# Key and value biases carried by tokens plus one, and new costs and shifts in the list schedule of a convolution, attention and expert kernel

## The chip, the cores and the metric

The kernel runs on one core of one Trainium2 chip. The metric is the device time of one execution in microseconds (us). All arithmetic is in fp32.

## The reference, cut to what matters

The input x has 32 images of 128 channels and 64 x 64 pixels. Layer 0 normalises groups of channels, convolves by a learned butterfly transform, and adds the result to x. Layer 1 takes each image as 4096 tokens of 128 channels. It adds attention over channels and then a mixture of eight experts, of which each token uses two. The part that the change touches is the attention:

```python
def _L1_attn_ref(x, Wk, bk, Wv, bv):
    k = x @ Wk.T + bk
    v = x @ Wv.T + bv
    scores = jnp.einsum('sbe,sbf->sef', k, v)
    probs = jax.nn.softmax(scores / jnp.sqrt(jnp.float32(seq_len)), axis=-1)
    return jnp.einsum('sef,sbf->sbe', probs, x)
...
t = t + _L1_attn_ref(_ln_t(t), L1_attn_Wk, L1_attn_bk, L1_attn_Wv, L1_attn_bv)
```

The "sequence" of this attention is the batch of one image's tokens: k and v have 128 features, and the scores are the 128 x 128 matrix k^T v, summed over the 4096 tokens. So with G the sum over tokens of the outer product of a normalised token with itself (the Gram matrix), the scores are Wk G Wv^T plus terms with the biases and with the sum of the tokens. A normalised token (`_ln_t`) has mean zero over its 128 channels.

## The kernel before, in words

The kernel has three phases. The first (until about 900 us in the trace) normalises and transforms the images, the second (until about 2560 us) mixes channels for each frequency, and the third, from line 727, does the inverse transform, the attention and the experts. Only the third is changed. Its work is written as small pieces for each image b, handed to a planner (`Plan`, lines 28 to 81) by `add` (line 805).

A piece has an engine, a cost in us, a due time, pieces that must be over before it, and counted resources that it takes or frees: `tl` (three PSUM banks for small products), `pe` (three PSUM banks for experts), `cv` (one PSUM tile of the inverse transform), `tm` (two buffers of gated expert outputs), `x`, `r`, `xg`, `xn`, `xT` and so on. `Plan.run` is a list schedule: it advances a clock by the costs, and when an engine is free it issues the ready piece with the earliest due time. The order that comes out is the order of the instructions on each engine; the chip then runs each engine's instructions in that order, with semaphores between engines. The costs and due times thus set nothing but an order. The due time is `SLOT` (114 us) times a position in images, plus an entry of `SHIFT` (line 797) by the piece's name, so a larger shift puts a piece later in rank.

For image b the pieces of the third phase are, in order of the data:

- `w`, `wo`, `h`, `ho` (lines 833 to 884): the inverse transform on PE into `cv`, copies `u` on ACT (line 848), and the addition onto the image `y` on DVE (line 868).
- `pt`, `to`, `sa` (913 to 942): four transposes at a time on PE turn the image to tokens, ACT copies them to `tk`, DVE takes statistics. `tk` has two buffers by b % 2, so `pt` of b waits for the output transposes `st` of b-2 (line 940).
- `va`, `pwa`, `na` (895 to 950): moments on DVE, a power on POOL (tile `m`, line 911), and minus mean times the reciprocal deviation on DVE (line 948, `nmr`).
- `xg`, `pg` (954 to 979): ACT writes the normalised tokens, a group of four blocks of 128 tokens at a time, and PE adds up the Gram matrix over 32 blocks. The buffers `xg` have a 129th column of ones, so the product of 128 x 129 also holds the sum of the tokens.
- `gs`, `pa`, `rows`, `pb`, `t1`, `pb2` (981 to 1008): DVE copies the Gram matrix to `gs`. `pa` is three matmuls that make two rows on one partition: the sum of the tokens, and that sum times Wv plus 4096 times the value bias (`ntok` holds 4096). DVE copies them to `rows`. `pb` is the Gram matrix times Wv plus an outer product of the first row and the value bias (lines 998 and 999, the second with a contraction of one row); DVE copies it to `t1`; `pb2` multiplies by Wk and adds an outer product of the key bias and the second row (1007 and 1008).
- `sm`, `pr`, `sr`, `sn`, `pc`, `prx` (1010 to 1049): the softmax, its transpose, and its product with the router weights.
- `pp`, `at`, `ad` (1052 to 1101): the attention's output by PE, scaled on ACT with `rstd` and `nmr`, added to `tk` on DVE, with statistics again.
- `vb`, `pwb`, `lg`, `nb` and `l2` to `gt` (1113 to 1175): the second power on POOL, router logits and the gates of the two best experts, on DVE.
- `xn`, `px`, `xT` (1180 to 1203), `pe` (line 1209, 64 for each image), `m` (the gated product `tm`, DVE line 1220), `s` (sums over experts on POOL, lines 1245 to 1248), `st` and `so` (transpose and store). In the last image five pairs of blocks are weighed on DVE alone (line 1232).

The set-up (lines 736 to 792) loads the weights on ACT's queue and takes the mean over input channels out of the expert weights, adding a 128th of the expert bias: with `nmr` of the experts raised by one (line 1126), tokens plus one times these weights give the product and the bias. The experts therefore already work in the way that the change brings to key and value.

Of the kernel before, what the change touches and what calls it, by code (L numbers as in the profile page):

```python
# [16 lines left out]
P = 128  # L17
# [73 lines left out]
def kernel(  # L91
# [644 lines left out]
    ct = ctx.enter_context(tc.tile_pool(name="ct", bufs=1))  # L736
    wk_sb = ct.tile([P, P], F32, name="wk_sb")
    nc.scalar.dma_start(wk_sb, wkT)
    wv_sb = ct.tile([P, P], F32, name="wv_sb")
    nc.scalar.dma_start(wv_sb, wvT)  # L740
    bk_sb = ct.tile([1, P], F32, name="bk_sb")
    nc.scalar.dma_start(bk_sb, bk.unsqueeze(0))
    bv_sb = ct.tile([1, P], F32, name="bv_sb")
    nc.scalar.dma_start(bv_sb, bv.unsqueeze(0))
    rb_sb = ct.tile([P, NE], F32, name="rb_sb")
# [6 lines left out]
    for e in range(NE):  # L752
        nc.gpsimd.memset(rank[:, e : e + 1], float(NE - e))
    ntok = ct.tile([1, 1], F32, name="ntok")
    nc.gpsimd.memset(ntok, float(NPIX))
    ones = ct.tile([P, P], F32, name="ones")
    nc.gpsimd.memset(ones, 1.0)

    NG = 4
    xg = [ct.tile([P, 4, P + 1], F32, name=f"xg{i}") for i in range(NG)]  # L760
    for t in xg:
        nc.gpsimd.memset(t[:, :, P : P + 1], 1.0)

# [8 lines left out]
    with tc.tile_pool(name="prep", bufs=1) as prep:  # L772

        ebb = prep.tile([P, NE, P], F32, name="ebb")
        nc.scalar.dma_start(
            ebb.rearrange("p e c -> p (e c)"), expert_b.rearrange("e c -> (e c)").partition_broadcast(P)
        )
        om = prep.tile([P, P], F32, name="om")
        nc.gpsimd.memset(om, 1.0 / P)
        for half in range(2):  # L780
            es = slice(4 * half, 4 * half + 4)
            pe = eps.tile([P, 512], F32, tag="pe", name=f"pm{half}")
            nc.tensor.matmul(pe, om, ew_sb[:, es, :].rearrange("d e c -> d (e c)"), start=True, stop=True)
            nc.vector.scalar_tensor_tensor(
                ebb[:, es, :].rearrange("p e c -> p (e c)"), ebb[:, es, :].rearrange("p e c -> p (e c)"),
                1.0 / P, pe, ALU.mult, ALU.subtract,
            )
        nc.vector.tensor_add(ew_sb, ew_sb, ebb)

        pe = eps.tile([P, 512], F32, tag="pe", name="pms")  # L790
        nc.tensor.matmul(pe[:, 0:NE], ones, prx[0][:, P + NE : QX], start=True, stop=True)
        nc.vector.tensor_copy(rws, pe[:, 0:NE])
# [4 lines left out]
    SHIFT = {  # L797
        "ad": 0.75, "at": -0.21, "f": 0.63, "gt": 0.63, "h": -0.15, "ho": -1.5, "l": 0.63, "lg": 0.15,
        "m": -0.08, "na": -0.08, "pe": 0.49, "pg": -0.45, "pt": -0.03, "pwa": -0.08, "pwb": 0.15,
        "r": -0.33, "s": 0.1, "sa": 0.33, "so": -0.09, "st": 0.47, "to": 0.52, "va": -0.08, "vb": 0.15,  # L800
        "wo": 0.12, "x": 0.44, "xT": 0.44, "xg": 0.12, "xn": 0.35,
    }
# [29 lines left out]
    def conv(b):  # L832
# [40 lines left out]
        for e in range(8):  # L873
            at = b + 0.08 * e
            add(b, f"w{e}", "PE", 1.8, at, w_inverse(e), [f"r{e}"] + [(b - 1, f"h{k}") for k in range(4)], ("cv",), ("r",))
            for oh in range(2):
                add(
                    b, f"wo{e}_{oh}", "ACT", 1.2, at, w_out(e, oh),
                    [f"w{e}"] + [(b - 1, f"h{k}") for k in range(4)], (), ("cv",) if oh else (),
                )  # L880
        for g in range(4):
            at = b + 0.68 + 0.07 * g
            add(b, f"h{g}", "PE", 2.15, at, h_inverse(g), [f"wo{e}_{oh}" for e in range(8) for oh in range(2)], ("cv",))
            add(b, f"ho{g}", "DVE", 1.25, at, h_out(g), [f"h{g}", "x"], (), ("cv",))

    def front(b):
# [8 lines left out]
        def moments(which):  # L895

            bs = v["bs"]
            even, odd = bs[:, :, 0, :], bs[:, :, 1, :]
            m2 = st.tile([P, 5, NT], F32, name=f"m2{which}_{b}", tag=f"m2{which}", bufs=2)
            total, diff, var, nmr, rstd = (m2[:, k, :] for k in range(5))  # L900
            nc.vector.tensor_add(total, even[:, :, 1], odd[:, :, 1])
# [36 lines left out]
        for g in range(8):  # L938
            at = s1 + 0.016 * g
            add(b, f"pt{g}", "PE", 0.55, at, turn(g), [(b - 2, f"st{g}")] + [f"ho{k}" for k in range(4)], ("tl",))  # L940
            add(b, f"to{g}", "ACT", 0.6, at, turned(g), [f"pt{g}"], (), ("tl",))
            add(b, f"sa{g}", "DVE", 1.15, at, stats1(g), [f"to{g}"] + (["sa0"] if g else []))
# [3 lines left out]
        def nmr1():  # L946
            total, var, nmr, rstd = v[1]
            nc.vector.scalar_tensor_tensor(nmr, total, -0.5, rstd, ALU.mult, ALU.mult)

        add(b, "na", "DVE", 0.9, s1 + 0.14, nmr1, ["pwa"])  # L950

        def norm(g):
            def run():
                total, var, nmr, rstd = v[1]
                for k in range(4):
                    i = 4 * g + k
                    nc.scalar.activation(
                        xg[g % NG][:, k, 0:P], t[:, i, :], AF.Identity, bias=nmr[:, i : i + 1], scale=rstd[:, i : i + 1]  # L960
                    )
            return run

        def gram(g):
            def run():
                if g == 0:
                    v["pg"] = tps.tile([P, 512], F32, tag="tl", name=f"pg{b}")
                for k in range(4):
                    i = 4 * g + k
                    nc.tensor.matmul(  # L970
                        v["pg"][:, 0 : P + 1], xg[g % NG][:, k, 0:P], xg[g % NG][:, k, :],
                        start=(i == 0), stop=(i == NT - 1),
                    )
            return run

        for g in range(8):
            at = s1 + 0.26 + 0.016 * g
            add(b, f"xg{g}", "ACT", 1.7, at, norm(g), ["na", (b if g >= NG else b - 1, f"pg{(g - NG) % 8}")], ("xg",))
            add(b, f"pg{g}", "PE", 1.06, at, gram(g), [f"xg{g}"] + ([f"pg{g - 1}"] if g else []), ("tl",) if g == 0 else (), ("xg",))

        def gsum():
            v["gs"] = st.tile([P, P + 1], F32, name=f"gs{b}", tag="gs")
            nc.vector.tensor_copy(v["gs"], v["pg"][:, 0 : P + 1])

        def rows_mm():
            pa, gs = tps.tile([P, 512], F32, tag="tl", name=f"pa{b}"), v["gs"]
            nc.tensor.matmul(pa[0:1, 0:P], gs[:, P : P + 1], ident, start=True, stop=True)
            nc.tensor.matmul(pa[0:1, P : 2 * P], gs[:, P : P + 1], wv_sb, start=True, stop=False)
            nc.tensor.matmul(pa[0:1, P : 2 * P], ntok, bv_sb, start=False, stop=True)
            v["pa"] = pa  # L990

        def rows_out():
            v["rows"] = st.tile([1, 2 * P], F32, name=f"rows{b}", tag="rows")
            nc.vector.tensor_copy(v["rows"], v["pa"][0:1, 0 : 2 * P])

        def kv1():
            pb = v["pb"] = tps.tile([P, 512], F32, tag="tl", name=f"pb{b}")
            nc.tensor.matmul(pb[:, 0:P], v["gs"][:, 0:P], wv_sb, start=True, stop=False)
            nc.tensor.matmul(pb[:, 0:P], v["rows"][:, 0:P], bv_sb, start=False, stop=True)

# [4 lines left out]
        def kv2():  # L1005
            pb = v["pb"]
            nc.tensor.matmul(pb[:, P : 2 * P], wk_sb, v["t1"], start=True, stop=False)
            nc.tensor.matmul(pb[:, P : 2 * P], bk_sb, v["rows"][:, P : 2 * P], start=False, stop=True)

# [28 lines left out]
        add(b, "gs", "DVE", 0.3, at, gsum, ["pg7"], (), ("tl",))  # L1038
        add(b, "pa", "PE", 0.9, at, rows_mm, ["gs"], ("tl",))
        add(b, "rows", "DVE", 0.42, at, rows_out, ["pa"], (), ("tl",))  # L1040
        add(b, "pb", "PE", 0.7, at, kv1, ["rows"], ("tl",))
        add(b, "t1", "DVE", 0.3, at, kv1_out, ["pb"])
        add(b, "pb2", "PE", 0.7, at, kv2, ["t1"])
        add(b, "sm", "DVE", 0.5, at, soft1, ["pb2"])
# [45 lines left out]
        for j, lo in enumerate(range(0, NT, 3)):  # L1090
            m = min(3, NT - lo)
            at = s1 + 0.45 + 0.016 * j
            add(b, f"pp{lo}", "PE", 0.3 * m, at, product(lo, m), ["prx", (b - 1, "lg")], ("tl",), ("x",) if lo == 30 else ())
            add(
# [82 lines left out]
    def experts(b):  # L1177
# [88 lines left out]
        for g in range(8):  # L1266
            at = s2 + 0.125 * g
            add(b, f"xn{g}", "ACT", 1.7, at - 0.1, normal(g), ["nb"], ("xn",))
            add(b, f"px{g}", "PE", 0.55, at - 0.05, turn(g), [f"xn{g}"], ("tl", "xT"), ("xn",))
            add(b, f"xT{g}", "ACT", 0.6, at - 0.05, turned(g), [f"px{g}"], (), ("tl",))  # L1270
            for k in range(4):
# [15 lines left out]
                elif k % 2:  # L1287
# [3 lines left out]
                    )  # L1291
            add(b, f"st{g}", "PE", 0.55, at + 0.25, back(g), [f"s{2 * g}", f"s{2 * g + 1}"], ("tl",))
            add(b, f"so{g}", "ACT", 0.6, at + 0.25, store(g), [f"st{g}"], (), ("tl",))
# [61 lines left out]
```

## Time and profile before

| | |
|---|---|
| median of three runs | 6177.5 us (6176.5 to 6183.15) |
| the profiled execution | 6179.07 us, span 6177.3 us, granted clock 0.99 |
| PE busy | 5988.3 us, 97% of the span |
| DVE, ACT, POOL busy | 4213.0, 3759.2, 4187.1 us |
| phase 1, 2 and the start of 3 | 0 to 900, 900 to 2560, 2560 to 2720 us |
| PE busy from 2560 to 2720 | 108.59 of 160 us |
| PE busy from 5600 to 6000, 6000 to the end | 382.24, 153.71 us |
| the Gram sum `pg` (lines 970, from 2700 on) | 1984 instructions, mean 275 ns |
| copies `gs`, `rows`, `t1` on DVE | mean 294, 412, 292 ns |
| `nmr` of the attention, line 948 | mean 558 ns |

In the profile, PE is TensorE, DVE is VectorE, ACT is ScalarE, POOL is GpSimd. Durations of PE instructions overlap, since matmuls are pipelined, so a mean is longer than what one adds to a busy stretch. One fp32 matmul is two instructions in the trace, and a transpose is one. Lines are named by the tile that is written, then those that are read: `pe<-ew_sb,xT`. Buffer numbers are left out, so one name stands for all images.

### The profile page before, as it was taken

The page shows a single profiled execution, that of the slowest core. Times are in us where ns is not written, and L with a number is a line of the kernel's source. Part 1 is how long each engine was busy: PE and PEld are TensorE (multiplying, and loading weights), DVE is VectorE, ACT ScalarE, POOL GpSimd, SP SyncE. Part 2 cuts the span into 40 slices and gives each one's busy share as a digit, 9 for nine tenths or more (in the row PEclk, how much of TensorE's full clock was granted, in tenths as well). Part 3 has the DMA queues.
Part 4 walks back from the last instruction along what each step waited for, and adds up shares of the span by engine and source line. Part 5 has one row for each costly group of instructions (what it writes and reads, how often), then busy time and mean ns, then how long its engine had stood idle before and what let it go on. Part 6 is the DMA issues. An engine that isn't in the chain of part 4 may idle for free. (4 is left out here: it accounts for less than half of the span.)

```text
span 6177.3 us, 218388 instructions
## 1 busy us (share of the span) xinstructions
PE 5988.3 (97%) x94922; PEld 4714.0 (76%) x94922; DVE 4213.0 (68%) x7686; ACT 3759.2 (61%) x7089; POOL 4187.1 (68%) x3755
## 2 busy tenths in 40 slices
PE   7999999999999999789999999999999999999988
PEld 7999998999999999666666666666666666666654
DVE  5565545555555555358778787787878778787777
ACT  7666654555555555376666666766667666666753
POOL 2110006666666666238888888888888888888888
PEclk9999999999999999899999999999999999999999
DMA  6766666666666666622222222222212222131100
GB/s 201 236 227 232 233 213 170 173 172 171 174 172 172 172 172 172 160 74 95 69 84 78 65 96 64 88 76 71 91 62 94 67 86 78 64 96 64 67 21 26
DMA packets 556965, 756.55 MB, mean 122 GB/s; under 512 B 58466, under 2 KB 321892, under 8 KB 551908
## 3 DMA queue, kind: packets, MB, share of 16 engines
q1 hardware_dynamic: 554096, 741.38, 39.9%
q8 instruction: 745, 12.21, 0.9%
q14 instruction: 216, 1.77, 0.1%
q10 hardware_dynamic: 1908, 1.19, 0.1%
HBM read 406.80 MB, written 335.54 MB: 120 GB/s over the span
## 5 line engine op out<-in xcount | busy, mean ns | idle before, releaser
L1209 PE MATMUL pe<-ew_sb,xT 128*128 128x512 f32 x4096 | 1984.6, 601 | 44.8 <-DVE tm L1220 40.6
L1220 DVE TENSOR_TENSOR tm<-pe,oh 128x512 f32<-128x512 f32 x2028 | 1341.2, 684 | 535.0 <-PE pe L1209 422.4
L1245 POOL TENSOR_TENSOR tm<-tm 128x512 f32<-128x512 f32 x1014 | 1296.3, 1293 | 314.6 <-DVE tm L1220 263.4
L1209 PEld LDWEIGHTS pe<-ew_sb,xT 128*128 128x128 f32 x4096 | 691.0, 191 | 518.7 <-issue 333.1
L621 DVE COPY f<-g 128x1024 f32<-128x1024 f32 x512 | 627.2, 1225 | 665.7 <-PE g L610 665.7
L632 PE MATMUL m<-f,s 128*64 128x64 f32 x32768 | 1071.3, 224 | 5.0 <-POOL s L583 3.6
L632 PEld LDWEIGHTS m<-f,s 128*64 128x64 f32 x32768 | 1000.7, 138 | 66.8 <-POOL s L583 3.9
L583 POOL COPY s<-l 128x512 f32<-128x512 f32 x512 | 546.5, 1102 | 599.2 <-issue 518.7
L621 ACT COPY f<-g 128x1024 f32<-128x1024 f32 x512 | 518.5, 1013 | 576.9 <-PE g L610 550.3
L1248 POOL TENSOR_TENSOR tk<-tk,tm 128x256 f32<-128x256 f32 x1014 | 753.4, 743 | 79.5
L848 ACT COPY u<-pu 64x512 f32<-64x512 f32 x1024 | 594.1, 580 | 308.3 <-PE pu L838 285.0
L1246 POOL TENSOR_TENSOR tm<-tm 128x512 f32<-128x512 f32 x507 | 647.0, 1276 | 39.8
L838 PEld LDWEIGHTS pu<-qw,r 128*128 128x128 f32 x4096 | 503.6, 196 | 170.1 <-ACT u L848 92.2
L610 PE MATMUL g<-c,wst 9*128 9x128 f32 x16384 | 609.2, 284 | 4.6 <-ACT f L621 3.4
L838 PE MATMUL pu<-qw,r 128*128 128x128 f32 x4096 | 522.6, 282 | 63.3 <-ACT u L848 52.9
L610 PEld LDWEIGHTS g<-c,wst 9*128 9x128 f32 x16384 | 510.9, 187 | 40.6 <-ACT f L621 4.5
L344 POOL TENSOR_TENSOR grstd<-gms,mhalf 128x1 f32<-128x1 f32 x32 | 17.8, 555 | 735.6 <-DVE gms L340 735.6
L585 POOL TENSOR_SCALAR s<-l 128x512 f32<-128x512 f32 x256 | 509.5, 1990 | 0.0
L413 PE MATMUL pf<-ph,v 128*128 128x128 f32 x4096 | 491.4, 278 | 5.2 <-ACT z L378 1.1
L1261 ACT COPY so<-po 128x512 f32<-128x512 f32 x256 | 150.9, 590 | 563.0 <-issue 411.9
L893 DVE BATCH_NORM_STATS2 bs<-tk 128x6 f32<-128x128 f32 x2048 | 448.2, 279 | 56.3 <-ACT tk L924 44.2
L413 PEld LDWEIGHTS pf<-ph,v 128*128 128x128 f32 x4096 | 467.1, 192 | 15.1 <-ACT z L378 7.1
(166 smaller groups left out, 8499.9 us busy)
## 6 DMA issues: line engine op xcount, KB each, us to landing
xf<-f SPq DMA_DIRECT2D x512, 256.0 KB, 3.3
l<-xf SPq DMA_DIRECT2D x1024, 128.0 KB, 3.3
pf<-o SPq DMA_DIRECT2D x1024, 128.0 KB, 3.3
r<-pf SPq DMA_DIRECT2D x512, 256.0 KB, 4.8
x<-in_x_dram SPq DMA_DIRECT2D x256, 256.0 KB, 4.6
y<-in_x_dram SPq DMA_DIRECT2D x32, 2048.0 KB, 8.1
out_dram<-so SPq DMA_DIRECT2D x256, 256.0 KB, 2.1
tw<-in_tw_dram SPq DMA_DIRECT2D x6, 384.0 KB, 6.6
```

The source lines that it names most:

```text
L413: nc.tensor.matmul(pl[:, j * P : (j + 1) * P], vs[b][:, 8 * g + j, :], ph.rearrange("h r m -> h (r m)"), start=True, stop=True,)
L583: nc.gpsimd.tensor_copy(dst, src)
L610: nc.tensor.matmul(pg[g // 2][:, g % 2, m * P : (m + 1) * P], wst[rows, 16 * half + 4 * t + m, :], c[rows].rearrange("r h k -> r (h k)"), ...
L621: copy(f.rearrange("i m (g o) -> i m g o", g=2), tile_of["g", w, half, t][k].rearrange("i g (o m) -> i m g o", o=4))
L632: nc.tensor.matmul(ps[hh * n : (hh + 1) * n, q, :], s[:, h].rearrange("i k b -> i (k b)")[:, B * r : B * r + n], f[:, h, r, :], start=(r = ...
L838: nc.tensor.matmul(ps[:, k, :], rs[b, e][:, k * P : (k + 1) * P], qw.rearrange("w r m -> w (r m)"), start=True, stop=True,)
L848: nc.scalar.copy(u[r * n : (r + 1) * n, :, oh * n + 8 * e : oh * n + 8 * e + 8], ps[oh * n : (oh + 1) * n, :, r * n : (r + 1) * n].rearran ...
L1209: nc.tensor.matmul(ps, tile_of["xT", b, i // 4][:, i % 4, :], ew_sb[:, es, :].rearrange("d e c -> d (e c)"), start=True, stop=True,)
L1220: nc.vector.tensor_tensor(tile_of["tm", b, i // 2][:, i % 2, es, :], tile_of.pop(("pe", b, i, half)).rearrange("p (e c) -> p e c", c=P), t ...
L1245: nc.gpsimd.tensor_tensor(tm[:, k, 0:4, :], tm[:, k, 0:4, :], tm[:, k, 4:8, :], ALU.add)
L1246: nc.gpsimd.tensor_tensor(tm[:, :, 0:2, :], tm[:, :, 0:2, :], tm[:, :, 2:4, :], ALU.add)
L1248: nc.gpsimd.tensor_tensor(t[:, lo : lo + 2, :], t[:, lo : lo + 2, :], tm[:, :, m, :], ALU.add)
```

## The change

Key and value take the form that the experts have. `na` gets a second operation that writes `nmr` plus one into a new slice `above`, and `xg` uses it as its bias, so the buffers hold normalised tokens plus one. Both weights lie in one tile `wkv`; in the set-up, the mean over input channels is taken out of them and a 128th of the bias is added. The product of tokens plus one with them is then the product with the old weights plus the bias. The 129th column, `ntok`, `pa`, `rows` and the two matmuls with one row go, and `pb` waits for `gs` alone. The rows `nmr` for `at` and the logits stay as they were.

The planner's costs of several pieces on PE are changed, and the table of shifts is replaced. `SLOT`, the resources and the dependences of all other pieces stay.

```diff
-    wk_sb = ct.tile([P, P], F32, name="wk_sb")
-    nc.scalar.dma_start(wk_sb, wkT)
-    wv_sb = ct.tile([P, P], F32, name="wv_sb")
-    nc.scalar.dma_start(wv_sb, wvT)
-    bk_sb = ct.tile([1, P], F32, name="bk_sb")
-    nc.scalar.dma_start(bk_sb, bk.unsqueeze(0))
-    bv_sb = ct.tile([1, P], F32, name="bv_sb")
-    nc.scalar.dma_start(bv_sb, bv.unsqueeze(0))
+    wkv = ct.tile([P, 2, P], F32, name="wkv")
+    nc.scalar.dma_start(wkv[:, 0, :], wkT)
+    nc.scalar.dma_start(wkv[:, 1, :], wvT)
...
-    xg = [ct.tile([P, 4, P + 1], F32, name=f"xg{i}") for i in range(NG)]
-    for t in xg:
-        nc.gpsimd.memset(t[:, :, P : P + 1], 1.0)
+    xg = [ct.tile([P, 4, P], F32, name=f"xg{i}") for i in range(NG)]
...
+        kvb = prep.tile([P, 2, P], F32, name="kvb")
+        nc.scalar.dma_start(kvb[:, 0, :], bk.partition_broadcast(P))
+        nc.scalar.dma_start(kvb[:, 1, :], bv.partition_broadcast(P))
+        pe = eps.tile([P, 512], F32, tag="pe", name="pmk")
+        nc.tensor.matmul(pe[:, 0 : 2 * P], om, wkv.rearrange("d e c -> d (e c)"), start=True, stop=True)
+        nc.vector.scalar_tensor_tensor(
+            kvb.rearrange("p e c -> p (e c)"), kvb.rearrange("p e c -> p (e c)"), 1.0 / P, pe[:, 0 : 2 * P],
+            ALU.mult, ALU.subtract,
+        )
+        nc.vector.tensor_add(wkv, wkv, kvb)
...
     SHIFT = {
-        "ad": 0.75, "at": -0.21, "f": 0.63, "gt": 0.63, "h": -0.15, "ho": -1.5, "l": 0.63, "lg": 0.15,
-        "m": -0.08, "na": -0.08, "pe": 0.49, "pg": -0.45, "pt": -0.03, "pwa": -0.08, "pwb": 0.15,
-        "r": -0.33, "s": 0.1, "sa": 0.33, "so": -0.09, "st": 0.47, "to": 0.52, "va": -0.08, "vb": 0.15,
-        "wo": 0.12, "x": 0.44, "xT": 0.44, "xg": 0.12, "xn": 0.35,
+        "ad": 0.66, "at": 0.51, "f": 0.63, "gs": 0.06, "gt": 0.63, "h": -0.18, "ho": -0.67, "l": 0.63,
+        "lg": 0.51, "m": -0.1, "na": -0.13, "nb": -0.7, "pb": 0.06, "pc": 0.06, "pe": 0.38, "pg": 0.11,
+        "pp": 0.23, "pr": 0.06, "prx": 0.06, "pt": -0.16, "pwa": -0.13, "pwb": 0.51, "px": 0.09, "r": -0.37,
+        "s": 0.46, "sa": 1.15, "sm": 0.06, "sn": 0.06, "so": -0.41, "sr": 0.06, "st": 0.99, "t": 0.06,
+        "to": 0.55, "va": -0.13, "vb": 0.51, "wo": 0.09, "x": 0.76, "xT": 0.76, "xg": 0.12, "xn": 0.6,
     }
...
+            nc.vector.tensor_scalar_add(v["above"], nmr, 1.0)
...
-                        xg[g % NG][:, k, 0:P], t[:, i, :], AF.Identity, bias=nmr[:, i : i + 1], scale=rstd[:, i : i + 1]
+                        xg[g % NG][:, k, :], t[:, i, :], AF.Identity, bias=v["above"][:, i : i + 1], scale=rstd[:, i : i + 1]
...
-                        v["pg"][:, 0 : P + 1], xg[g % NG][:, k, 0:P], xg[g % NG][:, k, :],
+                        v["pg"][:, 0:P], xg[g % NG][:, k, :], xg[g % NG][:, k, :],
...
-            nc.tensor.matmul(pb[:, 0:P], v["gs"][:, 0:P], wv_sb, start=True, stop=False)
-            nc.tensor.matmul(pb[:, 0:P], v["rows"][:, 0:P], bv_sb, start=False, stop=True)
+            nc.tensor.matmul(pb[:, 0:P], v["gs"], wkv[:, 1, :], start=True, stop=True)
...
-            nc.tensor.matmul(pb[:, P : 2 * P], wk_sb, v["t1"], start=True, stop=False)
-            nc.tensor.matmul(pb[:, P : 2 * P], bk_sb, v["rows"][:, P : 2 * P], start=False, stop=True)
+            nc.tensor.matmul(pb[:, P : 2 * P], wkv[:, 0, :], v["t1"], start=True, stop=True)
...
-        add(b, "pa", "PE", 0.9, at, rows_mm, ["gs"], ("tl",))
-        add(b, "rows", "DVE", 0.42, at, rows_out, ["pa"], (), ("tl",))
-        add(b, "pb", "PE", 0.7, at, kv1, ["rows"], ("tl",))
+        add(b, "pb", "PE", 0.35, at, kv1, ["gs"], ("tl",))
         add(b, "t1", "DVE", 0.3, at, kv1_out, ["pb"])
-        add(b, "pb2", "PE", 0.7, at, kv2, ["t1"])
+        add(b, "pb2", "PE", 0.35, at, kv2, ["t1"])
```

The other costs, old to new: `w` 1.8 to 1.9, `h` 2.15 to 2.05, `pt`, `px` and `st` 0.55 to 0.48, `pg` 1.06 to 0.9, `pp` 0.3 to 0.26 for each block, and on DVE `na` 0.9 to 1.2.

## The prediction before the run

> **What bounds the kernel now.** I read four views, in this order. First the page's shares: PE is busy 97% of the span, POOL and DVE 68%, ACT 61%, but these are means over three phases. The diff touches only the last phase, which starts near 2560 us of 6177.3. So second, the table by stages, cut at the `pa` matmuls of five images (the first matmuls behind the Gram sum):
>
> ```profile
> core 0: us, PE busy (x) PEld busy (x) DVE busy (x) ACT busy (x) POOL busy (x), PEclk, DMA share, GB/s
> 4072.30:4181.29 108.99, 107.78 (x755) 72.83 (x755) 85.05 (x189) 72.45 (x168) 95.57 (x83) 1.00 0.24 78
> 4181.29:5162.74 981.45, 970.30 (x6779) 655.40 (x6779) 766.12 (x1701) 651.97 (x1504) 859.56 (x739) 1.00 0.24 78
> 5162.74:5925.60 762.86, 754.48 (x5272) 509.73 (x5271) 594.97 (x1323) 507.18 (x1170) 668.84 (x575) 1.00 0.22 71
> ```
>
> One image, nine images, seven images: 108.99, 109.05 and 108.98 us each. PE is busy 1832.57 of 1853.30 us, 98.9%, at a granted clock of 1.00; POOL 87.6%, DVE 78%, DMA 24%. So a microsecond of TensorE work taken out here should come out of the span, as long as nothing else steps forward. Third, what PE waited for from 2720 to 5600:
>
> ```profile
> PE pu L838 <- ACT u L848: 18.5, 53, 2.6
> PE pe L1209 <- DVE tm L1220: 16.4, 26, 0.7
> ```
>
> With 0.3 us of another wait that is 35 us in 26 images. PE does not wait for the attention chain at all: while that chain goes from engine to engine, PE works on expert matmuls (`pe`) of the image before. Fourth, the timeline of PE at the place that is edited (start, length, line, operation, count; two instructions are one fp32 matmul; lengths overlap, so I use the distance of the starts and call it a slot):
>
> ```profile
> 4070.91 0.60 PE L1196 MATMUL px<-ident,xn 128*128 128x128 f32 x4
> 4071.34 1.02 PE L1209 MATMUL pe<-ew_sb,xT 128*128 128x512 f32 x2
> 4072.30 0.38 PE L987 MATMUL pa<-ident,gs 128*1 128x128 f32 x2
> 4072.51 0.38 PE L988 MATMUL pa<-wv_sb,gs 128*1 128x128 f32 x2
> 4072.83 0.38 PE L989 MATMUL pa<-bv_sb,ntok 1*1 1x128 f32 x2
> 4073.13 1.13 PE L1209 MATMUL pe<-ew_sb,xT 128*128 128x512 f32 x2
> 4074.09 0.38 PE L998 MATMUL pb<-wv_sb,gs 128*128 128x128 f32 x2
> 4074.41 0.48 PE L999 MATMUL pb<-bv_sb,rows 1*128 1x128 f32 x2
> 4074.82 1.13 PE L1209 MATMUL pe<-ew_sb,xT 128*128 128x512 f32 x2
> 4075.78 0.38 PE L1007 MATMUL pb<-t,wk_sb 128*128 128x128 f32 x2
> 4076.10 0.48 PE L1008 MATMUL pb<-rows,bk_sb 1*128 1x128 f32 x2
> 4076.51 3.70 PE L1209 MATMUL pe<-ew_sb,xT 128*128 128x512 f32 x8
> 4080.05 0.27 PE L1031 MATMUL pc<-ident,pr 128*128 128x128 f32 x1
> ```
>
> The reader is to see that no idle time stands in this stretch: each tiny matmul pushes an expert matmul back.
>
> **Part 1, matmuls removed.** From 4071.34 to 4080.05 are 8.71 us. In it lie 1+1+1+4 = 7 `pe` matmuls, worth 0.86 us each where a plain neighbour follows (`pe` at 4064.32, `pg` at 4065.18). 8.71 - 7 x 0.86 = 2.69 us is the attention block: 0.83 for the three `pa`, 2 x 0.73 for `pb` and its second half, 4 x 0.10 where a `pe` next to it starts or ends late. Afterwards two matmuls stay. At the slot of L998 (0.32) with three boundaries of 0.10 they cost 0.94, so 1.75 goes. If nothing slows their loads (0.22 as eight instructions of `pu` take 0.89, one boundary), they cost 0.54 and 2.15 goes. I take 1.80, near the first, since its slot is from the same instruction. The Gram matmul goes from 129 to 128 columns: eight instructions take 0.90 (4058.17 to 4059.07), eight of `pu` with 128 columns 0.89 (sixteen in 1.78): 0.01 x 8 = 0.08, between 0 and 0.1; I take 0.06. Together 1.86 us an image.
>
> The Trainium skill's page "TensorE: Matmul & The Clock Gate", section "Step-by-step: what each phase is for", speaks for a smaller gain: a stream of matmuls costs only its columns, since the next weights load behind the running matmul. By that rule the five removed matmuls of 128 columns would cost what plain ones cost here, 5 x 0.22 = 1.1 us an image, an estimate of 33 us in 30 images in place of the 54 that 1.80 gives, and the time would be about 6136. The trace shows 0.41 for L999, so I keep the slots.
>
> PE is packed for images 1 to 30 (`pa` of image 30 at 5925.60): 30 x 1.86 = 55.8 us. Image 0 runs alone at the start, where its chain from `pa` (2663.40) to `pb` (2666.80) takes 3.4 us, but the stage also waits for ACT's copies `u`; image 31 runs when POOL paces the end, and its `pa` to `pb` takes 1.79 (6029.65 to 6031.44). Between 0 and 3.4, and 0 and 2.6 with its bias slots: I take 1.5 each, 3 in all.
>
> **Part 2, what is added.** The mean of the weights adds one matmul of 256 columns in the set-up; the two like it with 512 columns took 0.86 per instruction at 2570 (the clock was low), so two halves cost 0.86. It stands on PE ahead of the rest of image 0's first `pu` block (2573.49), so I count 1 us, between 0 and 4 if it waits for a late weight load (these landed in 3.4 and 3.5 us). The two bias loads, the combination and the addition stand on ACT's queue and on DVE, which is idle from 2575.4 to 2611.9 but for waits: nothing. If that cover were gone, two more DMA issues (0.23 to 1.03 each on ACT's queue) and 0.7 us. `na` gets a second operation of 128x32: rows of that kind last 0.15 to 0.76, the nearest (L1126) 0.31. It lengthens the way to `xg`, and behind it on DVE queue the gated products; PE has expert matmuls in that time, and `rows` (0.41 on DVE) goes. Nothing in the packed images, 0.5 in the first and the last together. Sum of parts 1 and 2: -55.8 - 3 + 1.5 = -57.3, a span of 6120.
>
> **Part 3, the order.** The new costs and shifts change the order in which the same work is issued, and no row shows that. What can be won: 35 us of PE idle in 2720 to 5600, of 51.4 in 2560 to 2720 and 41 behind 5600 perhaps a third. What can be lost is as much again, or more (rival 3). One reason leans to a gain: the old costs add up to 112.1 us of PE an image where the profile has 107.8, the new ones to 106.7 where 105.9 will be left, so the list schedule now sees how near POOL is (its own costs 98.4). The 16.4 us in which `pe` waited for DVE are collisions that it could not see; I take a third of them, -5.5. Span 6114.5; the profiled run took 6179.07 around 6177.3, while the median of the runs is 6177.5, so the forecast is 6115 for the median. Its own band is 6100 to 6140.
>
> **Rivals.** (1) The order is worth much more: half of the 35 us and 10 to 25 of start and end go as well, 6078 to 6100. For it: the waits are short and regular, one a few times an image. Against: the last 180 us are paced by POOL and DVE. (2) PE is freed but POOL holds the pace. Sixteen sums of 5.42 us (4053.85 to 4059.29 is one) and two powers of 5.8 are 98.3 us of the 109. From 2900 to 5900 POOL stood idle for 266 us, 202.7 of them for DVE's products, 9.7 an image:
>
> ```profile
> POOL tm L1245 <- DVE tm L1220: 202.7, 169, 1.9
> POOL tm L1245 <- DVE sm L1024: 44.3, 27, 1.7
> POOL m L911 <- DVE m L906: 18.8, 55, 0.3
> ```
>
> These waits follow from PE's pace and should shrink with it; if two thirds of the gain sticks in them the time is 6140 to 6165. (3) Slower: the new shifts put the transposes back (`st`, +0.99 slots) later, and image b's first transposes (`pt`) wait for those of image b-2, which shares its buffer. From the last `pt` (4041.2) to the gates (4141.3) are 100 us, and two periods are 218, so the experts have 118 us where POOL needs 98.3: about 20 us to spare. Each microsecond beyond costs half a microsecond an image. With `pt` 24 us later the gain is used up; at 30 the image costs 5 - 1.9 = 3.1 more, 6270. As a band 6190 to 6280. Against it: the schedule places work by readiness, and a low rank matters only where PE has better work ready. (4) Gain and new waits cancel: 6165 to 6190.
>
> **How the numbers follow.** Forecast 0.52, rival 1 0.20, rival 2 0.13, rival 3 0.10, rival 4 0.05. The range 6080 to 6165 leaves out rivals 3 and 4 and the low edge of 1, 0.18 together. Faster by over 0.2% (below 6165; that is about what a measurement of this kernel can tell from no change): 0.52 + 0.20 + 0.13 = 0.85; within 0.2%: 0.05; slower: 0.10.
>
> **What would show it.** Right: from one image's `pb` to the next 107.0 to 107.3 us in the middle, PE again 98.5% busy or more, two matmuls of about 0.3 between `pe` blocks and no `rows`, PE's waits from 2720 to 5600 at or below 35 us, POOL's share there near 89%. Rival 2 would show PE below 98% with longer waits for DVE's `tm` and POOL never idle for long; rival 3 POOL idle for the gates once an image. The forecast is wrong if the period moves by something other than the removed slots, or if start and end move by over 20 us.

## The result, and the profile after

The changed kernel takes 6130.35 us (median of three runs, 6128.92 to 6131.49) against 6177.5: a ratio of 0.9922, with a 95% interval from 0.9903 to 0.9942. The profiled execution has a span of 6128.6 us, 48.7 less than before. A second measurement of the same kernel beside the last experiment gave 0.9918 (0.9904 to 0.9931). So it is faster, as forecast, inside the range (6080 to 6165) and inside the likeliest case's own band (6100 to 6140), but by 47 us where 62 were forecast.

The first view is the timeline of PE around `pb` in the changed kernel (start, length, line, operation, count):

```profile
4054.71 1.02 PE L1199 MATMUL pe<-ew_sb,xT 128*128 128x512 f32 x2
4055.57 0.38 PE L992 MATMUL pb<-wkv,gs 128*128 128x128 f32 x2
4055.79 1.88 PE L1199 MATMUL pe<-ew_sb,xT 128*128 128x512 f32 x4
4057.51 0.38 PE L1000 MATMUL pb<-t,wkv 128*128 128x128 f32 x2
4057.73 2.74 PE L1199 MATMUL pe<-ew_sb,xT 128*128 128x512 f32 x6
```

Each of the two matmuls left takes a slot of 0.22 us, and the expert matmuls around them take their plain 0.43 per instruction: the boundaries of 0.10 are gone as well. The block costs 0.44 where it cost 2.69. From one `pb` to the next are now 107.4 to 108.0 us (4055.57 to 4163.47 is one), about 107.65, against 109.0.

The second view is what PE waited for from 2720 to 5600 in the changed kernel (total, times, longest):

```profile
PE pe L1199 <- DVE tm L1210: 48.2, 52, 1.5
PE py L863 <- ACT u L851: 15.9, 25, 0.9
PE pu L841 <- ACT u L851: 2.5, 1, 2.5
```

The wait of the expert matmuls for DVE has grown from 16.4 to 48.2 us, and the inverse transform along h (`py`) waits where it did not; the wait of `pu` for ACT fell from 18.5 to 2.5. The third view is the middle of the phase as one stage, from 2900 to 5300, in the changed kernel; behind the length stand the busy times of PE, its weight loads, DVE, ACT and POOL, then the granted clock:

```profile
2900.00:5300.00 2400.00, 2342.61 (x16506) 1600.49 (x16505) 1930.69 (x4215) 1626.78 (x3724) 2121.16 (x1827) 1.00 0.26 81
```

PE is busy 97.6% here, not 98.5%, and POOL 88.4%. In the same stretch before, PE was busy 2372.32 us, 98.8%. Taken by the image (the share times the distance of the `pb`), PE's work went from 107.7 to 105.1 us and its idle time from 1.26 to 2.57. So 2.6 us of work left each image, and 1.3 us of new waiting took half of it back.

Where the 48.7 us of the span came from, by the starts of the 32 `pb`: to the first +1.0 (2666.80 to 2667.80), images 0 to 2 -4.5, the 28 distances in the middle -39.5, the last distance -8.1 (104.04 to 95.93), and from the last `pb` to the end +2.3.

### The profile page after: what moved, and what is told of

It is laid out like the page before. It is cut to its first block, busy times and chain, and to the rows that moved or that the text cites. A ratio compares the mean times of both kernels' runs of the same rounds, so it can differ in the third digit from the quotient of the medians.

```text
span 6128.6 us, 217668 instructions
## 1 busy us (share of the span) xinstructions
PE 5913.9 (96%) x94604; PEld 4689.9 (77%) x94604; DVE 4246.3 (69%) x7688; ACT 3768.5 (61%) x7089; POOL 4177.1 (68%) x3750
## 4 chain that ended last, share of the span: by engine, by line
PE 81%; DVE 10%; ACT 4%; DMA 2%; issue 2%; POOL 1%; SPq 0%; ACTq 0%; POOLq 0%; DVEq 0%
PE pe L1199 23%; PE m L632 17%; PE g L610 9%; PE pf L413 7%; PE pu L841 5%; PE py L863 4%; PE pp L1048 4%; PE pg L975 4%; PE pv L391 3%; DVE tm L1210 2%; PE px L1186 2%; DMA out_dram<-so 2%; DVE eq L1123 1%; ACT u L851 1%; PE pz L368 1%
## 5 line engine op out<-in xcount | busy, mean ns | idle before, releaser
L1061 ACT ACTIVATE pp<-pp,m 128x128 f32<-128x128 f32 x1024 | 441.1, 431 | 143.1 <-PE pp L1048 119.5
L916 POOL TENSOR_TENSOR m<-m,mhalf 128x32 f32<-128x32 f32 x64 | 348.4, 5443 | 203.6 <-DVE m L911 203.6
```

## Experiments

Ratios are to the kernel before, measured beside each run; the distance of the `pb` is in the middle of the phase, and PE's idle time is that from 2720 to 5600.

| run | median us | ratio (95% interval) | distance of `pb`, us | PE idle, us |
|---|---|---|---|---|
| before | 6177.5 | 1 | 109.0 | 35.0 |
| changed kernel | 6130.4 | 0.9922 (0.9903 to 0.9942) | 107.65 | 66.7 |
| same_order | 6111.7 | 0.9888 (0.9875 to 0.9902) | 106.89 | 32.5 |
| bias_old_plan | 6105.5 | 0.9881 (0.9867 to 0.9894) | 106.73 | 35.4 |
| order_only | 6370.4 | 1.0309 (1.0294 to 1.0323) | 114 to 116 | 147.4 |
| five_more | 6165.2 | 0.9974 (0.9964 to 0.9984) | 109.0 | 72.5 |
| new_costs | 6287.4 | 1.0166 (1.0152 to 1.0180) | 108 to 117 | 140.8 |
| new_shifts | 6335.1 | 1.0242 (1.0227 to 1.0257) | 72 and 158 in turn | 164.9 |
| five_one_row | 6185.2 | 1.0003 (0.9994 to 1.0012) | 109.4 | 72.8 |
| gate_lengths | 6334.9 | 1.0245 (1.0231 to 1.0259) | 112 to 115 | 167.4 |
| split_after | 6132.8 | 0.9903 (0.9886 to 0.9919) | 107.7 | 69.3 |
| split_bias | 6092.6 | 0.9841 (0.9826 to 0.9856) | 105.90 | 19.4 |
| pull_after | 6154.4 | 0.9948 (0.9936 to 0.9961) | 108.4 | 87.3 |
| after_again (the changed kernel once more) | 6137.4 | 0.9918 (0.9904 to 0.9931) | 107.9 | 74.8 |

Two executions of the changed kernel thus differ by 0.3 us in the distance and by 8 us in PE's idle time, all of it in the wait of `py` for ACT (15.9 and 24.0 us); in the new order, differences of that size mean little.

### The arithmetic alone, in the order of before

```diff
(on the changed kernel: SHIFT and all costs as before, and)
+        add(b, "pa", "PE", 0.9, at, lambda: None, ["gs"], ("tl",))
+        add(b, "rows", "DVE", 0.42, at, lambda: None, ["pa"], (), ("tl",))
+        add(b, "pb", "PE", 0.7, at, kv1, ["rows"], ("tl",))
```

> The bias part alone, in exactly the order of the kernel before: the planner still holds pieces named pa and rows with their old costs, but they issue nothing; costs and shifts are the old ones. Theory (order costs): the removed work is worth its slots, about 2.3 us an image with the boundaries gone, as in the changed kernel, and without the new order PE's idle time stays near 35 us from 2720 to 5600, so the period falls from 109.0 to about 106.9 and the time to about 6112, below the changed kernel. Rival (POOL and DVE hold the pace): PE's idle time grows by about 1.2 us an image here as well, period near 107.8, time near 6135.

Measured: 6111.7 us, ratio 0.9888, and 106.89 us from one `pb` to the next. The waits of PE from 2720 to 5600 are those of before to within 0.7 us (18.5 and 16.4 there):

```profile
PE pu L840 <- ACT u L850: 17.8, 55, 2.4
PE pe L1200 <- DVE tm L1211: 16.1, 26, 0.7
```

So in an unchanged order the arithmetic is worth 2.09 us an image and 64 us of span (6113.5 against 6177.3), with no new wait. The changed kernel has the same arithmetic and differs in nothing but the order; it is slower than this by 0.74 us an image, since in the new order PE's work is 0.6 us less and its waiting 1.3 us more. The 0.6 stand at places where unlike matmuls follow each other: in same_order the four transposes `px` take 0.53 us ahead of `py` (4027.55 to 4028.08) and 0.44 ahead of `pe` (4043.79 to 4044.23). With the starts added up over 20 images, `px` takes 0.3 us an image less in the new order and `pu` 0.2. The rival, that POOL and DVE hold the pace, falls.

### The arithmetic with the planner freed of the removed pieces

```diff
(against the planner of the kernel before; all other costs and SHIFT as there)
-        add(b, "pa", ...)
-        add(b, "rows", ...)
-        add(b, "pb", "PE", 0.7, at, kv1, ["rows"], ("tl",))
+        add(b, "pb", "PE", 0.35, at, kv1, ["gs"], ("tl",))
```

> The bias part with the pieces pa and rows taken from the planner and pb at 0.35, all other costs and all shifts as before. Theory (the new shifts and costs lose): 6105 to 6120, faster than the changed kernel. Rival (POOL and DVE hold the pace): 6130 or more, and the new shifts win nothing or little.

Measured: 6105.5 us, ratio 0.9881 (0.9867 to 0.9894), below the whole interval of the changed kernel. The new costs and shifts lose some 0.4% of the time against simply leaving them.

### The order alone, and its two halves

order_only is the kernel before with the new costs and shifts; new_costs and new_shifts are the new arithmetic with only one half of the new table each.

> The new costs and shifts alone on the old arithmetic: pa, rows and the bias products stay, with their old costs and the shift 0.06 of their neighbours. Theory (the new order costs about 1.2 us of idle time an image): 6190 to 6215, slower than the kernel before. Rival (the waits come from PE being faster, not from the order): 6170 to 6180, no change.

> The bias part with the new costs and the old shifts. Theory A (the shifts lose, the costs are harmless): 6100 to 6115, as with all old costs (6105). Theory B (costs and shifts each lose part): 6115 to 6130. If true costs alone help, below 6100.

> The bias part with the old costs and the new shifts. Theory A (the shifts lose): 6125 or more, at least as slow as the changed kernel; with costs that they were not made for, up to 6300, since the same shifts on the old arithmetic gave 6370. Theory B (the costs lose): 6105 to 6115.

Measured: 6370.4, 6287.4 and 6335.1 us, all slower than the kernel before. No forecast came near for the first two, and the third lies 35 us above the 6300 that was thought possible. The direction of the theory held for order_only, its size did not: not 10 to 35 us but 190. The reading of the two halves was wrong as a question: neither costs nor shifts "lose" by themselves, since with the same arithmetic either half alone (6287.4, 6335.1) is 157 to 230 us slower than both old (6105.5) or both new (6130.4). order_only is no clean measure of the order either, because pieces that the new shifts were not made for stand in it; same_order against the changed kernel is. In new_shifts images come in pairs, 72 us and 158 us apart, and PE waits for many things in turn; the three longest from 2720 to 5600:

```profile
PE py L863 <- DVE y L871: 32.4, 23, 1.7
PE pt L924 <- ACT so L1251: 29.1, 20, 3.0
PE pu L841 <- ACT u L851: 23.8, 15, 2.7
```

No single wait explains the 165 us of idle time there.

### Is PE still the limit, and what does a small matmul cost?

```diff
             nc.tensor.matmul(pb[:, 0:P], v["gs"], wkv[:, 1, :], start=True, stop=True)
+            for k in range(5):
+                nc.tensor.matmul(pb[:, 3 * P : 4 * P], v["gs"], wkv[:, 1, :], start=True, stop=True)
```

five_one_row has `v["gs"][0:1, :]` and `wkv[0:1, 1, :]` in the loop, a contraction of one row. Nothing reads these columns.

> The changed kernel with five more matmuls of 128x128 by 128x128 in each image's pb, into columns that nothing reads; the planner and so the order are the same. If PE is the limit, 5 x 0.22 = 1.1 us an image come on top, 31 x 1.1 = 34 us: 6164. If the pace is POOL's or DVE's by now, PE's 2.5 us of idle time an image take most of it: 6130 to 6145.

> The changed kernel with five more matmuls in each pb as in five_more, but with a contraction of one row in place of 128; same order. If a one-row matmul itself is dear (0.41 us as the slot of the old bias product), 5 x 0.41 = 2.05 us an image, 6130 + 31 x 2.05 = 6194. If it costs what a full one costs (1.28 us an image in five_more), 6165 again, and the old slot of 0.41 came from what stood around it.

Measured: 109.0 and 109.4 us from `pb` to `pb`, so 1.3 and 1.7 us an image more than the profiled execution of the changed kernel (1.0 and 1.4 more than that of after_again); 6165.2 and 6185.2 us. PE's idle time is 72.5 and 72.8 us, between the 66.7 and 74.8 of the changed kernel: the added work goes into the span in full, 34.8 us for 31 times 1.11. PE is the limit, although it idles about 2.5% of the time. Five matmuls of one row cost 0.4 us an image more than five full ones. The timelines of PE show where the difference stands; first five_more, then five_one_row:

```profile
4068.93 0.38 PE L992 MATMUL pb<-wkv,gs 128*128 128x128 f32 x2
4069.15 1.28 PE L994 MATMUL pb<-wkv,gs 128*128 128x128 f32 x10
4070.26 1.88 PE L1201 MATMUL pe<-ew_sb,xT 128*128 128x512 f32 x4
4071.98 0.38 PE L1002 MATMUL pb<-t,wkv 128*128 128x128 f32 x2
```

```profile
4074.76 0.39 PE L992 MATMUL pb<-wkv,gs 128*128 128x128 f32 x2
4075.07 1.38 PE L994 MATMUL pb<-wkv,gs 1*128 1x128 f32 x10
4076.38 1.98 PE L1201 MATMUL pe<-ew_sb,xT 128*128 128x512 f32 x4
4078.20 0.38 PE L1002 MATMUL pb<-t,wkv 128*128 128x128 f32 x2
```

Five full matmuls take 1.11 us and leave their neighbours alone (`pb` 0.22, four `pe` instructions 1.72). Five one-row matmuls take 1.31, and the matmul before and the one after each lose 0.10 (0.31 and 1.82). The 0.20 within the five lie at their two ends, as the last four and the last of the ten instructions show, each with the start of its first:

```profile
4075.84 0.60 PE L994 MATMUL pb<-wkv,gs 1*128 1x128 f32 x4
4076.18 0.27 PE L994 MATMUL pb<-wkv,gs 1*128 1x128 f32 x1
```

Three instructions take 0.34 us, 0.11 each as in a full matmul; the last one takes 0.20 (to 4076.38), and of the 0.77 us of the first six (4075.07 to 4075.84) likewise 0.1 is more than 6 x 0.11. So inside the row a one-row matmul costs 0.22 like a full one, and each passage between a full and a one-row operand costs about 0.2 us, 0.1 on the instruction ahead of it and 0.1 on the one behind. A single one between full ones pays both passages: 0.22 + 0.4. That is what the old bias products did, with 0.41 in their own slot and 0.10 on the neighbour on each side.

### Why the new order waits: the gate block on DVE

In the changed kernel PE waits 1.53 us once an image, at 4110.60, for a gated product. The timeline of DVE there, cut to the stretch ahead of it:

```profile
4102.48 0.68 DVE L1210 TENSOR_TENSOR tm<-pe,oh 128x512 f32<-128x512 f32 x1
4103.08 1.08 DVE L1128 TENSOR_TENSOR lg<-lg,m 128x256 f32<-128x256 f32 x1
...
4104.95 0.86 DVE L896 BATCH_NORM_STATS2 bs<-tk 128x6 f32<-128x128 f32 x4
4105.74 0.40 DVE L1121 TENSOR_REDUCE tops<-lg 128x32 f32<-128x256 f32 x1
...
4107.16 1.38 DVE L1123 TENSOR_TENSOR eq<-eq,rank 128x256 f32<-128x256 f32 x1
...
4109.87 0.68 DVE L1210 TENSOR_TENSOR tm<-pe,oh 128x512 f32<-128x512 f32 x1
```

The wait of PE ends with the last of these products:

```profile
4110.60 1.12 PE L1199 MATMUL pe<-ew_sb,xT 128*128 128x512 f32 x2 [1.53 <-DVE tm L1210]
```

For 6.8 us no gated product (`tm`) stands on DVE: the second step of the logits, a group of statistics and the search for the best expert (f1) follow each other, and the planner holds the search for 2.6 us where it takes 4.1. From this I made a theory and four tests.

```diff
(gate_lengths; in the same way f3 2.6 to 4.0, gt 3.2 to 4.0, nb 1.0 to 2.0)
-        add(b, "f1", "DVE", 2.6, ...)
+        add(b, "f1", "DVE", 4.0, ...)
...
(pull_after, where the pieces are issued in the planned order)
+            if kind == "gated":
+                run()
+                if rest:
+                    rest()
```

In split_after and split_bias the second half of f1 or f3 (`rest`) is issued behind a gated product, if that product is the next piece on DVE. In pull_after the statistics and the first half of f1 that follow l2 are held back behind the next product as well.

> The changed kernel with four costs on DVE set to what its own trace shows (f1 and f3 4.0 in place of 2.6, gt 4.0 for 3.2, nb 2.0 for 1.0); shifts unchanged. Theory (PE waits for the gated products since the schedule thinks the gate blocks on DVE shorter than they are): PE's wait for DVE from 2720 to 5600 falls from 48 us to 20 or 30, and the time to 6100 to 6120. Rival (the shifts were found for the old lengths, so any change of costs upsets the order): 6130 or more.

Measured: 6334.9 us. Truer lengths for four pieces of DVE made the order far worse. PE's wait for the gated products did fall, from 48.2 to 5.6 us, but `pu` then waited 101.8 us for ACT's copies: the theory was right on the wait and wrong on the time.

> The changed kernel in its own order, but each of the two searches for the best expert (f1 and f3, five operations on DVE) is issued in two halves with the next gated product between them, if that product is the next piece on DVE. Theory (PE waits because these blocks, over 4 us in a row, hold the gated product that frees a bank of PSUM for it): PE's wait for DVE from 2720 to 5600 falls from 48 us to 35 or less, the time to 6110 to 6122. Rival (the wait is set by POOL's pace, DVE's blocks only show where it lands): 6126 to 6134, the wait moves elsewhere.

Measured: ratio 0.9903, an interval that holds the changed kernel's 0.9918 and 0.9922; `pb` 107.7 us apart. The first wait fell from 1.53 to 0.64 us, but the second, 6.5 us later, rose from 0.36 to 1.02. The wait moved on, as the rival said. Its reason, POOL's pace, does not show: neither in the changed kernel nor here did DVE wait for POOL from 2720 to 5600.

> The same split in the kernel with the bias part and the old costs and shifts (6105). There PE waits for DVE 16 us from 2720 to 5600, once an image, next to such a block. Theory: this wait goes nearly, and the time falls by 10 to 16 us to 6089 to 6096. Rival: no change, 6100 to 6108.

Measured: ratio 0.9841 (0.9826 to 0.9856), `pb` 105.90 us apart instead of 106.73. In the old order the wait for DVE is gone; all that PE waits for from 2720 to 5600 is

```profile
PE pu L853 <- ACT u L863: 18.4, 55, 2.6
PE po L1266 <- ACT tk L941: 0.3, 1, 0.3
```

There the theory held: one wait of 0.6 us an image stood behind the search f3, and issuing a product in its middle removes it. By the ratios the gain is some 25 us, more than the 10 to 16 forecast; what the rest is was not traced. This is the fastest version of the study, 6092.6 us where the kernel before took 6190.7.

> The changed kernel in its own order with the split of f1 and f3, and with the statistics and the first half of f1 that follow l2 on DVE issued after the next gated product instead of before it, so that no stretch of over about 3 us on DVE there is without one (6.8 us in the changed kernel). Theory (the wait of 1.53 us an image stands behind that stretch): it goes, PE's wait for DVE from 2720 to 5600 falls to 25 us or less, the time to 6105 to 6118. Rival (DVE has too much to do in the whole stretch of the gates while POOL works, so the wait only moves on): 35 us or more, 6122 to 6134.

> The changed kernel once more, beside the one above on the same chip: 6125 to 6135, ratio 0.991 to 0.9935.

Measured: 0.9948 for pull_after, slower than after_again (0.9918) on the same chip, with 61.2 us of waiting for DVE. The product that was moved ahead waits for POOL, and PE's first wait, 1.36 us again, ends with the product after it. DVE's timeline, cut, and the row of PE (in brackets the idle time before, and its releaser):

```profile
4121.86 0.69 DVE L1250 TENSOR_TENSOR tm<-pe,oh 128x512 f32<-128x512 f32 x1 [0.62 <-POOL tk L1279]
4122.47 0.86 DVE L925 BATCH_NORM_STATS2 bs<-tk 128x6 f32<-128x128 f32 x4
...
4127.69 1.87 DVE L1250 TENSOR_TENSOR tm<-pe,oh 128x512 f32<-128x512 f32 x3
```

```profile
4128.42 2.84 PE L1239 MATMUL pe<-ew_sb,xT 128*128 128x512 f32 x6 [1.36 <-DVE tm L1250]
```

So the edit did not do what its expectation says: from 4122.47 to 4127.69 there are still 5.2 us without a product, because no product is the next piece behind the first half of f1. The theory in its strict form was not tested. What the traces show is narrower: moving one product ahead makes PE wait for the next one. In the changed kernel DVE itself is full there, busy 15.69 of the 16.00 us from 4102 to 4118. That fits the rival's reason, too much work on DVE in the whole stretch, though the time is worse than the rival forecast. Why the new order packs this work so densely stays open, since any change of a cost or shift gives a different order altogether.

## Why the prediction was right, and where it was wrong

**By its own signs.** The time lies in the range. `rows` is gone and POOL's share is near the 89% named, but three other signs of a right forecast did not come: 107.65 us from `pb` to `pb` and not 107.0 to 107.3, PE 97.6% busy and not 98.5%, 66.7 us of waiting and not 35. The distance moved by more than the removed slots, namely by new waits too, and the prediction had named that as a sign of being wrong.

**Bottleneck.** PE as the limit of images 1 to 30 was right and is shown: removed work comes out (same_order), added work goes in (five_more), with idle time as in the kernel that each is compared with.

**Part 1, size.** Forecast 1.86 us an image; 2.09 were measured in the same order (PE's work 107.7 to 105.7), and 2.6 of PE's work in the new one. The term that was too small is the attention block. I kept L998's slot of 0.32 and three boundaries of 0.10 for what stays, 0.94, and set 0.54 as the least. In the changed kernel it is 0.44: slot and boundaries came from the one-row and one-column neighbours, and left with them. So 2.25 went and not 1.80. In bias_old_plan the distance fell by just that, 108.98 to 106.73; in same_order, with one expert matmul between the two, about 0.17 of it stays in the block (a slot of 0.33 and 0.06 ahead of it). The Gram matmul's eight instructions take 0.89 (4151.63 to 4152.52), but before, unrounded, most such groups took 0.892 as well: with the starts added up over 20 images, the Gram sum takes 7.14 us an image before and 7.13 in same_order, so of the 0.06 taken for it 0.01 is there.

The rule that the prediction drew from the Trainium skill (page "TensorE: Matmul & The Clock Gate", section "Step-by-step: what each phase is for"), that a stream of matmuls costs only its columns, agrees with this trace inside a row of one kind, at 0.22 us a matmul of full or one-row operands. It gave 1.1 us for the five that were removed; the other 1.15 of the 2.25 were the passages between unlike operands, which only the trace showed.

**Part 2.** Nothing of the set-up or of the longer `na` can be seen in the middle of the phase. The first `pb` came 1.0 us later in the changed kernel (2.8 in after_again) and 2.6 earlier in same_order; shifts of this size at the start were not traced to a cause.

**Part 3, the failed step.** I argued: "One reason leans to a gain", the costs nearer to the truth let the schedule see POOL, and took -5.5 us. The runs show the opposite sign: at equal arithmetic the new order is slower by 0.74 us an image, 21 us over the 28 middle distances, given back in part by the last image (95.93, in same_order 103.87); in the span 15 us are left. The reason itself failed both times it was tried alone: the truer PE costs under the old shifts gave 6287 us, and truer DVE costs under the new shifts 6335. The step that failed is thus the wait: -5.5 us where PE waited 1.3 us an image more. Costs and shifts together only pick one order out of very many; a cost nearer to the truth does not make a better one.

**Rivals.** The trace of the changed kernel looks like rival 2: PE below 98%, with longer waits for `tm`. same_order shows that it is not, since POOL stands at 89.4% of 2900 to 5300 there (2145.53 us), without the waits. The signature that I had named for rival 2 could not tell it from a worse order. Rival 3 was right that the order could cost, but its mechanism, late transposes of image b, was not seen in the changed kernel. Rival 1, an order worth much more, is refuted by same_order; rival 4, gain and new waits cancelling, is partly true, for the new order took a quarter of the gain in the span (15 of 64 us). That the sum came out near is in part luck, because errors of opposite sign met: 2.09 instead of 1.86 gives 7 us more over 30 images, and part 3 some 21 to 26 us less. Together that is about the 15 us by which the time missed 6115.

## What to carry to other kernels

Where one engine is packed, read the price of an edit from the distance of the starts, with what the neighbours lose, and keep in mind that a boundary goes when its cause goes. When a change of arithmetic comes together with a new schedule, run the arithmetic in the old order first: here it was worth 1.1% alone, and the new schedule gave 0.3 to 0.4% back. In this kernel costs and priorities of the list schedule were a matched pair: three runs that changed one alone, even towards the truth, lost 157 to 230 us, so what such a change gives must be measured.

## What the runs showed of the hardware

A matmul with a contraction of one row costs the same 0.22 us as one of 128 rows when it stands in a row of its kind, but each passage between the two costs about 0.2 us, half on the instruction ahead and half on the one behind (five_one_row beside five_more). A one-row product alone between full ones therefore cost 0.6 us in the kernel before. I had taken the old slots as partly lasting.
